# Where a unit's first copy, its last result and the last output piece stand in their queues

## The chip, the core and the metric

The kernel runs on one core of one Trainium2 chip. Time is device time of one execution in microseconds (us). TensorE (PE) multiplies, VectorE (DVE) does elementwise arithmetic on two operands, ScalarE (ACT) does activation functions and plain copies, GpSimd (POOL) and SyncE (SP) here mostly issue DMA transfers. Each engine runs its own queue in order and waits on semaphores for the others.

## The reference

The input is x of 2048 tokens by 512 channels, float32. With `ln` a layer norm without gain and `h`, `hh` a layer norm with gain and bias and the same shifted by one token:

```python
x = ln(L0_attn_x)                                  # first layer, RWKV
k = (h*mk + hh*(1-mk)) @ Wk.T;  v = (h*mv + hh*(1-mv)) @ Wv.T;  r = (h*mr + hh*(1-mr)) @ Wr.T
x = x + sigmoid(r) * wkv(k, v, tm_first) @ Wo.T    # 512 x 512 matrices
kk = (h*ck + hh*(1-ck)) @ Wkey.T                   # 2048 x 512
x = x + sigmoid((h*cr + hh*(1-cr)) @ Wcr.T) * (silu(kk) @ Wval.T)
y = L0_attn_x + x                                  # second layer, gated FFN
gate, up = split(ln(y) @ w_gate_up.T)              # 2 x 2048 rows
out = y + (silu(gate) * up) @ w_down.T
```

Almost all of it is matrix products of 512-wide blocks.

## The kernel before

**Tiling.** Tokens come in four blocks of 512. A weight of 512 x 512 and a block of 512 tokens form one 512 x 512 x 512 product, a *unit*. It is not multiplied in eight quarter products but in seven, by a Strassen-Winograd scheme: quarters A11..A22 of the weight and sums S1..S4 of them, quarters B11..B22 of the activations and sums T1..T4. A quarter product is eight matmuls of 128x128 by 128x256; the profile counts them on line 546.

**One unit** (`unit`, L526). Three accumulators of one PSUM bank each take the products: `z`, `accv`, `accx`. Step 1 puts A11·B11 into `z`, and ACT copies it to `accv` (L564). Step 2 adds A12·B21 to `accv`, which is result (0,0), and `sink` uses it. Step 6 adds S2·T2 to `z`, copied to an SBUF tile `u2` (L574). Step 5 adds S1·T1, copied to `accx` (L578). Then step 7 (S3·T3, result (1,1) from `z`), step 3 (`accx`, result (0,1)) and step 4 (A22·T4; DVE adds `z` and `u2` for result (1,0)). `sink` differs by unit: an activation on ACT for gates, k, r and the hidden layers, an addition or a multiplication on DVE for the others.

**Interleaving of units.** Steps 7, 3 and 4 are *held* and popped between the next unit's steps, so PE's order around a unit's start is: step 5 of the unit before, step 4 of the one before that, **step 1 of this unit, step 7 of the unit before, step 2 of this unit**. Step 2 adds to `accv`, so it can't start before the ACT copy of step 1 has ended; one product lies between them.

**Order of the other engines.** PE, DVE and ACT run in the order in which the program text emits. After each product, `due` runs the functions that were `put_off` (`later(fn, n)` runs fn at the n-th `due`), and `tick` (L290) spends the length of the product (STEP, 1.72) on work from the lists `hot`, `background` and `preps`: norms, mixes (`mix<-hT`, an ACT scaling on L483 and a DVE step on L387), sums of activations (L379) and sums of weights (`raw`). What `tick` emits stands in the queues at that point.

**The FFN's down product** (`down_product`, L1114) takes the scheme twice: seven outer products n = 0..6, each of them seven inner products of four groups (`steps`, L1150; matmuls of 128x128 by 128x128 on L1165). Inside one outer product, `z` is one 128-column piece of a bank that accumulates A11·B11, S2·T2, S1·T1, S3·T3 and A22·T4; after each of the first four, `keep` (L1177) lets ACT copy it to an SBUF tile `r`, and the next product into `z` must wait for that copy. `y` takes A12·B21 and S4·B22. `rest` (L1200) and `seventh` (L1211) finish `r` on DVE; `summed` (L1117) adds the outer products up. Inner products six and seven of outer product n are held and popped after the first and the second inner product of n + 1. For the last token block `sink` (L1243) adds a 128x2x256 piece to the residual tile and SP stores it; the piece (1,0) is first given its other terms at n = 5, and at n = 6 the last one, then stored as one 256 KB transfer.

The program ends when that last store has landed.

Of the kernel before, what the change touches and what calls it, by code (L numbers as in the profile page):

```python
# [11 lines left out]
ALU = mybir.AluOpType  # L12
# [3 lines left out]
P = 128  # L16
# [4 lines left out]
HB = TB // 2  # L21
# [38 lines left out]
def rwkv_ffn_kernel(  # L60
# [145 lines left out]
    def later(fn, ticks=1):  # L206
        put_off.append([ticks - 1, fn])
# [76 lines left out]
    def due():  # L284
        for item in put_off:
            item[0] -= 1
        while put_off and put_off[0][0] < 0:
            put_off.popleft()[1]()

    def tick(length=STEP):  # L290
        for item in preps:
            item[1] -= 1
        slack[0] = max(min(slack[0] + SHARE * length - spent[0], 2.5), -2.5)
        spent[0] = 0.0
        credit[0] = min(credit[0] + credit[1], 2.0)
        while slack[0] > 0 and (hot or background or preps):
            go = False
            if preps and credit[0] >= 1 and prep_one():
                credit[0] -= 1
                go = True  # L300
            elif hot or background:
                go = run_one(False)
            slack[0] -= spent[0]
            spent[0] = 0.0
            if not go:
                break

    def push(name, gen, ready=None):
        background.append([ready, gen, name, False, background])
# [68 lines left out]
    def tt(out, a, b, op):  # L378
        nc.vector.tensor_tensor(out, a, b, op)  # L379
        cost(size(out))  # L380
# [145 lines left out]
    def unit(weights, Bs, sink, by_token, done=None, free=None, loose=False):  # L526

        acc, tmp = {}, {}  # L530
        last = len(weights) - 1

        def product(z, a, b, first=False, between=None, part=None):
            if first:
                acc[z] = bank()
            pz = acc[z]
            groups = list(range(last + 1) if part is None else part)
            for g in groups:
                wg = weight(weights[g], a)
                act = Bs[g][b]  # L540
                for m in range(2):
                    for k in range(2):
                        lo = slice(m * P, (m + 1) * P)
                        lhsT = act[:, k, lo] if by_token else wg[:, k, lo]
                        rhs = wg[:, k, :] if by_token else act[:, k, :]
                        mm = nc.tensor.matmul(  # L546
                            pz[:, m, :],
                            lhsT=lhsT,
                            rhs=rhs,
                            start=first and g == 0 and m == 0 and k == 0,  # L550
                            stop=g == last and k == 1,
                            skip_group_check=True,
                        )
                latest[:] = [mm.ins.name]
                due()
                if g < groups[-1]:
                    tick()
                    if between is not None and g < 2:
                        between()

        def step1():
            product("z", A11, B11, True, pop_held)
            acc["v"], acc["x"] = accv, accx
            nc.scalar.copy(accv, acc["z"])  # L564

        def step2(part=None):
            product("v", A12, B21, part=part)
            if part is None or last in part:
                sink(0, 0, accv)

        def step6():
            product("z", S2, T2)
            tmp["u2"] = u_tile("u2")
            nc.scalar.copy(tmp["u2"], acc["z"])  # L574

        def step5():
            product("z", S1, T1)
            nc.scalar.copy(accx, acc["z"])  # L578
            if loose:
                tmp["u4"] = u_tile("u4")  # L580
                nc.scalar.copy(tmp["u4"], acc["z"])
            later(lambda: tt(tmp["u2"], tmp["u2"], accx, ALU.subtract), 1)

        def step7():
            if loose:
                product("y", S3, T3, True)
                tt(tmp["u4"], acc["y"], tmp["u4"], ALU.add)
                sink(1, 1, tmp["u4"])
                return
            product("z", S3, T3)  # L590
            sink(1, 1, acc["z"])

        def step3():
            product("x", S4, B22)
            sink(0, 1, accx)

        def step4():
            if loose:
                tt(tmp["u2"], tmp["u2"], tmp["u4"], ALU.add)
            product("z", A22, T4, loose)  # L600
            tt(tmp["u2"], acc["z"], tmp["u2"], ALU.add)
            sink(1, 0, tmp["u2"])
            if free is not None:
                free()
            if done is not None:
                later(done, 2)

        if last > 0:

            def most():  # L610
                step2(range(last))

            def rest():
                step2([last])

            order = (step1, None, most, step6, rest, step5)
        else:
            order = (step1, None, step2, step6, None, step5, None)
        for s in order:
            if s is None:  # L620
                pop_held()
            else:
                s()
                tick()
        held.extend(((STEP, step7), (STEP, step3), (STEP, step4)))
        if loose:
            release()
            flush()
# [485 lines left out]
    def down_product(b, sink, final):  # L1114
        base = {}

        def summed(n, r):  # L1117


            def add(o, i, j=None):  # L1120
                tt(base[o], base[i], r if j is None else base[j], ALU.add)

            if n == 0:
                base["p1"] = r
            elif n == 1:
                base["p3"] = r
            elif n == 2:
                base["u2"] = r
                add("u2", "u2", "p1")
            elif n == 3:  # L1130
                add("p1", "p1")
                sink(0, 0, base["p1"])
            elif n == 4:
                base["u4"] = r
                add("u4", "u4", "u2")
                add("p3", "p3", "u4")
                sink(0, 1, base["p3"])
            elif n == 5:
                add("u4", "u4")
                sink(1, 1, base["u4"])  # L1140
                add("u2", "u2")
                if final:
                    sink(1, 0, base["u2"])
            elif final:
                sink(1, 0, r, True)
            else:
                add("u2", "u2")
                sink(1, 0, base["u2"])

        def steps(n):  # L1150
# [25 lines left out]
            def keep(n, m):  # L1176
                nc.scalar.copy(st["r"][:, m, n * P : (n + 1) * P], st["z"])  # L1177
# [18 lines left out]
            def fifth():  # L1196
                product(st["z"], S1, T1, False)
                keep(0, 1)

                def rest():  # L1200
                    r = st["r"]
                    tt(r[:, 0, P:], r[:, 0, P:], r[:, 1, :P], ALU.subtract)
                    tt(r[:, :, :P], st["y"], r[:, :, :P], ALU.add)

                later(rest, 1)

            def sixth():
                product(st["z"], S3, "T3", False)
                keep(1, 1)

            def seventh():  # L1211
                product(st["z"], A22, T4, False)
                r = st["r"]
                tt(r[:, 0, P:], st["z"], r[:, 0, P:], ALU.add)
                if n + 2 < 7:
                    quarter_sums(b, n + 2)
                summed(n, r)
# [4 lines left out]
        for n in range(7):  # L1222
            t = DOWN[n][1]
            while (b, t if t != T3 else "T3") not in made:
                flush_one()
            one = steps(n)
            one[0]()
            tick(half)
            pop_held()
            one[1]()  # L1230
            tick(half)
            pop_held()
            for k in range(2, 5):
                one[k]()
                tick(half)
                if n == 0:
                    pop_held()
            held.extend((half, k) for k in one[5:])

    def ffn_down(b):  # L1240
        final = b == NB - 1

        def sink(i, j, c, last=False):  # L1243
            v = block_view(rs[b], i, j)
            tt(v, c, v, ALU.add)
            if final and (i, j) == (1, 0) and not last:
                return
            eng = nc.sync if final else nc.gpsimd
            eng.dma_start(  # L1249
                out_t[b][:, 2 * j : 2 * j + 2, i * HB : (i + 1) * HB],  # L1250
                rs[b][:, 2 * j : 2 * j + 2, i * HB : (i + 1) * HB],
            )

        down_product(b, sink, final)

# [157 lines left out]
```

## Time and profile before

| | |
|---|---|
| median of 3 runs | 1256.92 us (1256.81 to 1257.21) |
| profiled execution, its own time | 1256.11 us |
| its span on the core | 1254.3 us |
| TensorE clock granted | 1.0 throughout |
| ACT copies `accv<-ps` (L564) | 64, 571 ns each |
| ACT copies `u<-ps` (L574), `accx<-ps` (L578) | 64 each, 585 and 571 ns |
| DVE `TENSOR_TENSOR` 128x512 | 685 to 692 ns |
| DVE `TENSOR_TENSOR` 128x128, 128x256 | 289 to 292 ns, 425 ns |
| ACT `ACTIVATE` 128x512 from an SBUF tile, from PSUM | 630 ns, 597 ns |
| last store, 256 KB, issue to landing | 2.2 us |

The span is the time between the first and the last instruction; 1.8 us of the profiled execution lie outside it. A row of a timeline gives start, duration, engine, line, operation, output and inputs, and in brackets how long the engine had been idle and who released it. Ends of matmuls are modelled by the profiler, so distances between matmuls are taken here from start to start.

### The profile page before, as it was taken

The page shows a single profiled execution, that of the slowest core. Times are in us where ns is not written, and L with a number is a line of the kernel's source. Part 1 is how long each engine was busy: PE and PEld are TensorE (multiplying, and loading weights), DVE is VectorE, ACT ScalarE, POOL GpSimd, SP SyncE. Part 2 cuts the span into 40 slices and gives each one's busy share as a digit, 9 for nine tenths or more (in the row PEclk, how much of TensorE's full clock was granted, in tenths as well). Part 3 has the DMA queues.
Part 4 walks back from the last instruction along what each step waited for, and adds up shares of the span by engine and source line. Part 5 has one row for each costly group of instructions (what it writes and reads, how often), then busy time and mean ns, then how long its engine had stood idle before and what let it go on. Part 6 is the DMA issues. An engine that isn't in the chain of part 4 may idle for free.

```text
span 1254.3 us, 18161 instructions
## 1 busy us (share of the span) xinstructions
PE 1238.0 (99%) x6588; PEld 1109.2 (88%) x6588; DVE 702.6 (56%) x1319; ACT 355.8 (28%) x656; POOL 151.1 (12%) x276
## 2 busy tenths in 40 slices
PE   8999999999999999999999999999999999999998
PEld 7888888888888888888888888998899988998898
DVE  5867566467674665722562265555546455462466
ACT  5433263142522334302311232212221132212211
POOL 2122221222121222222210000000000000000000
PEclk9999999999999999999999999999999999999999
DMA  5666777888778877798865655895559855785575
GB/s 188 233 195 211 244 249 244 249 292 282 241 259 257 290 251 248 248 334 309 254 211 178 221 145 151 247 345 164 144 173 302 280 151 150 234 291 165 152 220 200
DMA packets 137959, 288.55 MB, mean 230 GB/s; under 512 B 17296, under 2 KB 18320, under 8 KB 136848
## 3 DMA queue, kind: packets, MB, share of 16 engines
q1 hardware_dynamic: 115424, 215.53, 56.1%
q0 software_dynamic: 21440, 70.27, 15.4%
q10 hardware_dynamic: 1008, 1.59, 0.3%
q8 instruction: 53, 0.87, 0.3%
q14 instruction: 34, 0.28, 0.1%
HBM read 245.39 MB, written 41.94 MB: 229 GB/s over the span
## 4 chain that ended last, share of the span: by engine, by line
PE 95%; ACT 3%; DVE 2%; issue 1%; DMA 0%; POOL 0%; ACTq 0%; DVEq 0%; POOLq 0%
PE ps L546 49%; PE ps L1165 14%; PE accv L546 11%; PE accx L546 10%; PE ps L656 8%; PE ps L430 2%; ACT mix L483 1%; PE warm L337 1%; DVE u L379 1%; DVE mix L387 0%; DMA w<-in_w 0%; ACT e L877 0%; ACT x L740 0%; ACT r L878 0%; ACT accv L564 0%
## 5 line engine op out<-in xcount | busy, mean ns | idle before, releaser
L546 PE MATMUL ps<-zT,w 128*128 128x256 f32 x1280 | 289.5, 379 | 0.7 <-ACT u L574 0.7
L546 PEld LDWEIGHTS ps<-zT,w 128*128 128x128 f32 x1280 | 241.8, 190 | 33.2 <-ACT u L574 1.1
L546 PE MATMUL ps<-mix,w 128*128 128x256 f32 x880 | 201.0, 379 | 0.0
L546 PEld LDWEIGHTS ps<-mix,w 128*128 128x128 f32 x880 | 167.0, 190 | 22.6
L379 DVE TENSOR_TENSOR u<-u,accx 128x512 f32<-128x512 f32 x64 | 43.9, 686 | 118.3 <-ACT accx L578 118.3
L1165 PE MATMUL ps<-w,hid 128*128 128x128 f32 x832 | 104.7, 275 | 0.4 <-ACT r L1177 0.4
L1165 PEld LDWEIGHTS ps<-w,hid 128*128 128x128 f32 x832 | 99.8, 192 | 1.3 <-ACT r L1177 0.5
L546 PE MATMUL ps<-w,t 128*128 128x256 f32 x432 | 96.5, 379 | 0.0
L546 PEld LDWEIGHTS ps<-w,t 128*128 128x128 f32 x432 | 81.9, 190 | 11.1
L1165 PE MATMUL ps<-w,quads 128*128 128x128 f32 x704 | 89.2, 275 | 0.4 <-ACT r L1177 0.4
L656 PE MATMUL ps<-mix,w 128*128 128x256 f32 x384 | 85.1, 380 | 3.7 <-DVE mix L387 3.7
L656 PEld LDWEIGHTS ps<-mix,w 128*128 128x128 f32 x384 | 72.3, 190 | 14.6 <-DVE mix L387 5.1
L1165 PEld LDWEIGHTS ps<-w,quads 128*128 128x128 f32 x704 | 84.3, 192 | 0.9 <-ACT r L1177 0.5
L379 DVE TENSOR_TENSOR u<-ps,u 128x512 f32<-128x512 f32 x65 | 44.9, 691 | 66.3 <-PE ps L546 66.3
L578 ACT COPY accx<-ps 128x512 f32<-128x512 f32 x64 | 36.5, 571 | 153.0 <-PE ps L546 152.9
L379 DVE TENSOR_TENSOR raw<-raw 128x512 f32<-128x512 f32 x92 | 63.3, 688 | 29.1 <-DMA raw<-d 10.0
L564 ACT COPY accv<-ps 128x512 f32<-128x512 f32 x64 | 36.5, 571 | 140.5 <-PE ps L546 140.5
L1177 ACT COPY r<-ps 128x128 f32<-128x128 f32 x112 | 29.8, 266 | 142.7 <-PE ps L1165 142.7
L574 ACT COPY u<-ps 128x512 f32<-128x512 f32 x64 | 37.5, 585 | 112.9 <-PE ps L546 112.9
L1249 POOL DMA_DIRECT2D out<-resid x12 | 8.6, 716 | 476.9 <-DVE resid L379 476.9
L546 PE MATMUL accv<-zT,w 128*128 128x256 f32 x256 | 60.7, 380 | 0.7 <-ACT accv L564 0.7
L546 PE MATMUL accx<-zT,w 128*128 128x256 f32 x256 | 60.5, 379 | 0.0
(158 smaller groups left out, 1659.1 us busy)
## 6 DMA issues: line engine op xcount, KB each, us to landing
w<-sum SPq DMA_DIRECT2D x304, 256.0 KB, 3.3
w<-in_w SPq DMA_DIRECT2D x256, 256.0 KB, 3.3
w<-dd SPq DMA_DIRECT2D x112, 256.0 KB, 3.6
raw<-in_w POOLq DMA_DIRECT2D x48, 256.0 KB, 4.8
sum<-raw POOLq DMA_DIRECT2D x48, 256.0 KB, 3.8
w<-d SPq DMA_DIRECT2D x48, 256.0 KB, 3.3
q<-in_w POOLq DMA_DIRECT2D x36, 256.0 KB, 4.9
sum<-q POOLq DMA_DIRECT2D x36, 256.0 KB, 3.9
```

The costliest lines, as they stand in the source:

```text
L337: nc.tensor.transpose(pt[:, 0, 0:P], ident, ident)
L379: nc.vector.tensor_tensor(out, a, b, op)
L430: nc.tensor.transpose(flat[:, t * P : (t + 1) * P], h[:, t, c * P : (c + 1) * P], ident)
L483: nc.scalar.activation(dst(c), hT[:, c, 0:TB].rearrange("p (j t) -> p j t", j=2), AF.Copy, scale=onem[:, row - MK, c : c + 1],)
L546: mm = nc.tensor.matmul(pz[:, m, :], lhsT=lhsT, rhs=rhs, start=first and g == 0 and m == 0 and k == 0, stop=g == last and k == 1, skip_gro ...
L564: nc.scalar.copy(accv, acc["z"])
L574: nc.scalar.copy(tmp["u2"], acc["z"])
L578: nc.scalar.copy(accx, acc["z"])
L656: mm = nc.tensor.matmul(acc[i, j][:, m, :], lhsT=act[:, k, lo] if by_token else wg[:, k, lo], rhs=wg[:, k, :] if by_token else act[:, k, : ...
L1165: mm = nc.tensor.matmul(dst, lhsT=x[k][:, g, :], rhs=wt[:, g, :], start=first and g == 0, stop=g == 3, skip_group_check=True,)
L1177: nc.scalar.copy(st["r"][:, m, n * P : (n + 1) * P], st["z"])
L1249: eng.dma_start(out_t[b][:, 2 * j : 2 * j + 2, i * HB : (i + 1) * HB], rs[b][:, 2 * j : 2 * j + 2, i * HB : (i + 1) * HB],)
```

## The change

In `unit`: `product` gets an argument `read`, called when the last matmul of the product has been emitted and before `due`; step 1 hands in the copy to `accv`, which thus stands on ACT's queue ahead of everything that `due` runs. Step 4 no longer calls `sink(1, 0, ...)` itself, but puts it off to the next product's `due`, that is behind the copy. Step 4 also sets a flag, `quiet`, and the next `tick` takes nothing from `background`.

In the down product, only for the last block and n = 6: the third inner product (S2·T2) is emitted ahead of the held seventh of n = 5, and then the fifth (S1·T1) ahead of the fourth (S4·B22). `seventh` adds `r` to the output tile before its own product and stores three quarters of the piece; after its product one addition of 128x128 takes `z` straight from PSUM into the last quarter, which is stored.

```diff
+    quiet = [False]
     def tick(length=STEP):
...
-            elif hot or background:
+            elif hot or background and not quiet[0]:
                 go = run_one(False)
...
+        quiet[0] = False
...
-        def product(z, a, b, first=False, between=None, part=None):
+        def product(z, a, b, first=False, between=None, part=None, read=None):
...
                 latest[:] = [mm.ins.name]
+                if read is not None and g == groups[-1]:
+                    read()
                 due()
...
         def step1():
-            product("z", A11, B11, True, pop_held)
             acc["v"], acc["x"] = accv, accx
-            nc.scalar.copy(accv, acc["z"])
+            product(
+                "z", A11, B11, True, pop_held, read=lambda: nc.scalar.copy(accv, acc["z"])
+            )
...
             product("z", A22, T4, loose)
             tt(tmp["u2"], acc["z"], tmp["u2"], ALU.add)
-            sink(1, 0, tmp["u2"])
+            later(lambda: sink(1, 0, tmp["u2"]), 1)
             if free is not None:
                 free()
             if done is not None:
                 later(done, 2)
+            quiet[0] = True
...
                 if final:
-                    sink(1, 0, base["u2"])
-            elif final:
-                sink(1, 0, r, True)
+                    sink(1, 0, base["u2"], "first")
...
             def seventh():
+                r = st["r"]
+                if final and n == 6:
+                    sink(1, 0, r, "most")
                 product(st["z"], A22, T4, False)
-                r = st["r"]
+                if final and n == 6:
+                    sink(1, 0, st["z"], "last")
+                    return
                 tt(r[:, 0, P:], st["z"], r[:, 0, P:], ALU.add)
...
-            pop_held()
-            for k in range(2, 5):
+            if final and n == 6:
+                one[2]()
+                tick(half)
+                pop_held()
+                order = 4, 3
+            else:
+                pop_held()
+                order = 2, 3, 4
+            for k in order:
                 one[k]()
                 tick(half)
...
+        eng = nc.sync if final else nc.gpsimd
+        def store(tokens, cols):
+            eng.dma_start(out_t[b][:, tokens, cols], rs[b][:, tokens, cols])
-        def sink(i, j, c, last=False):
-            v = block_view(rs[b], i, j)
+        def sink(i, j, c, part=None):
+            tokens, cols = slice(2 * j, 2 * j + 2), slice(i * HB, (i + 1) * HB)
+            if part == "last":
+                tokens, cols = 0, slice(HB + P, 2 * HB)
+            v = rs[b][:, tokens, cols]
             tt(v, c, v, ALU.add)
-            if final and (i, j) == (1, 0) and not last:
-                return
-            eng = nc.sync if final else nc.gpsimd
-            eng.dma_start(
-                out_t[b][:, 2 * j : 2 * j + 2, i * HB : (i + 1) * HB],
-                rs[b][:, 2 * j : 2 * j + 2, i * HB : (i + 1) * HB],
-            )
+            if part is None or part == "last":
+                store(tokens, cols)
+            elif part == "most":
+                store(1, cols)
+                store(0, slice(HB, HB + P))
```

More of the change, by code (lines that the diff above doesn't have):

```diff
@@ L1198, in fifth, with rest @@
                 keep(0, 1)
-                def rest():
-                    r = st["r"]
-                    tt(r[:, 0, P:], r[:, 0, P:], r[:, 1, :P], ALU.subtract)
-                    tt(r[:, :, :P], st["y"], r[:, :, :P], ALU.add)
                 later(rest, 1)
+            def rest():
+                r = st["r"]
+                tt(r[:, 0, P:], r[:, 0, P:], r[:, 1, :P], ALU.subtract)
+                tt(r[:, :, :P], st["y"], r[:, :, :P], ALU.add)
             def sixth():
@@ L1211, in seventh @@
             def seventh():
+                r = st["r"]
+                if final and n == 6:
+                    sink(1, 0, r, "most")
                 product(st["z"], A22, T4, False)
-                r = st["r"]
+                if final and n == 6:
+                    sink(1, 0, st["z"], "last")
+                    return
                 tt(r[:, 0, P:], st["z"], r[:, 0, P:], ALU.add)
```

## The prediction

> **What bounds the kernel now.** First the busy shares:
>
> ```profile
> PE 1238.0 (99%) x6588; PEld 1109.2 (88%) x6588; DVE 702.6 (56%) x1319; ACT 355.8 (28%) x656; POOL 151.1 (12%) x276
> ```
>
> PE is never free for long, and the number of matmuls doesn't change. So the change can gain only where PE waits, and behind its last matmul. The waits of PE, longest first (total us, times, longest):
>
> ```profile
> PE accv L546 <- ACT accv L564: 3.8, 5, 1.0
> PE ps L656 <- DVE mix L387: 3.7, 4, 1.5
> PE ps L546 <- issue: 1.6, 1, 1.6
> PE warm L337 <- POOL ident masks.py:199: 1.4, 1, 1.4
> PE ps L1165 <- ACT r L1177: 0.7, 2, 0.4
> PE ps L546 <- ACT u L574: 0.7, 1, 0.7
> ```
>
> The first row is what the copy to `accv` costs: five waits in 64 units. Rows 2 to 4 lie before 112 us, where plain units and the start run; nothing is moved there. The fifth is the end of the program. No row names a DMA. I then looked at each of the five in the timeline. PE alone around the second:
>
> ```profile
> 261.40 7.07 PE L546 MATMUL ps<-mix,w 128*128 128x256 f32 x32
> 269.48 1.99 PE L546 MATMUL accv<-mix,w 128*128 128x256 f32 x8 [1.01 <-ACT accv L564]
> 271.31 1.89 PE L546 MATMUL ps<-mix,w 128*128 128x256 f32 x8
> ```
>
> and ACT alone at the same place:
>
> ```profile
> 266.43 0.63 ACT L877 ACTIVATE e<-r 128x512 f32<-128x512 f32 x1 [2.14 <-DVE r L383]
> 267.09 0.63 ACT L878 ACTIVATE r<-r 128x512 f32<-128x512 f32 x1
> 267.62 1.32 ACT L483 ACTIVATE mix<-hT_b,onem 128x512 f32<-128x512 f32 x2
> 268.85 0.57 ACT L564 COPY accv<-ps 128x512 f32<-128x512 f32 x1
> 269.37 1.32 ACT L483 ACTIVATE mix<-hT_b,onem 128x512 f32<-128x512 f32 x2
> ```
>
> The four products from 261.40 are step 5, step 4, step 1, step 7. Step 1 is done near 266.6, but the copy stands behind two exponentials (the result (1,0) of step 4, which waits for DVE) and two background mixes, and starts at 268.85. PE starts 0.06 us after its end: it is the copy that is waited for.
>
> **The unit part, step by step.** A product goes start to start in 1.727 us (256.22 to 261.40 is three of them). From the start of step 5 to the start behind step 2 are five products, 8.635 us if nothing stalls. Measured:
>
> - 161.77 to 171.59: 9.82, lost 1.19 (copy behind a silu that waited for DVE's `u`)
> - 261.40 to 271.31: 9.91, lost 1.28 (above)
> - 324.86 to 333.87: 9.01, lost 0.37 (silu)
> - 337.32 to 346.38: 9.06, lost 0.42 (silu)
> - 424.10 to 434.01: 9.91, lost 1.28 (exponentials and mixes, as above)
>
> Together 4.54 us, more than the 3.8 of the waits view since a stall also delays the weight load behind it.
>
> With the copy directly behind its product it waits only for PE. A copy starts 0.20 us behind the start of the following product (273.03 to 273.23 for `u`). In the second case step 1 ends at 261.40 + 3 x 1.727 = 266.58, the copy runs 266.78 to 267.35, and step 2 wants it at 268.31: 0.96 spare. In the first, third and fifth cases the same 0.96 holds, ACT being free at 165.1, 329.3 and 427.0; in the fourth three mixes end at 342.6 and the copy at 343.3, wanted at 344.2. So all five stalls go: **-4.54**.
>
> What is now late instead:
>
> - *The result (1,0) on ACT, in every unit.* The copy waits at the head of ACT's queue until step 1 has ended, and the activation stands behind. Counted from the end of step 4: copy 1.93 to 2.50, activation to 3.13 (0.63). The next ACT reader, step 7's result, is ready at 3.65. It fits with 0.5 spare; the activation's own reader (the next unit's multiplication, or sums of hidden quarters) is products away. Price 0.
> - *Background work held back one tick.* In the two long k/r/v stretches (from 262 and from 425 us) the mixes come behind the copy, and DVE does three or four mixes before the step that multiplies the exponentials, up to 2 us later than now. I followed DVE through with 0.6 to 0.75 per step. At 425 us the last v result (`e<-u,e`) ends near 454.2 and the second sum near 455.5, on a scale where PE is 1.28 earlier; the output unit wants them at 455.2 and 456.9. Spare 1.0 and 1.4; in the stretch from 262 us about 1.7 and 2. DVE has about 4 us of idle time between 429 and 453 that absorbs the delay. Price 0, at most 1 each if I am off by a DVE step or two.
> - *Sums of weights and of `zT`.* They move by one or two places on DVE, have tens of us, and GpSimd's order is unchanged; SP's is unchanged until the last block. Price 0.
>
> The units with no held steps (681.80 and 686.19) wait for a copy with nothing between; those stay.
>
> **The end, step by step.** The timeline now:
>
> ```profile
> 1243.12 1.95 PE L1165 MATMUL ps<-w,quads 128*128 128x128 f32 x16
> 1244.22 0.29 DVE L379 TENSOR_TENSOR r<-ps,r 128x128 f32<-128x128 f32 x1 [0.33 <-PE ps L1165]
> 1246.67 0.69 DVE L379 TENSOR_TENSOR resid<-r,resid 128x512 f32<-128x512 f32 x1
> 1247.21 1.16 PE L1165 MATMUL ps<-w,hid 128*128 128x128 f32 x8 [0.35 <-ACT r L1177]
> 1247.67 0.42 DVE L379 TENSOR_TENSOR r<-ps,r 128x256 f32<-128x256 f32 x1
> 1248.73 1.16 PE L1165 MATMUL ps<-w,quads 128*128 128x128 f32 x8 [0.35 <-ACT r L1177]
> 1249.92 0.29 DVE L379 TENSOR_TENSOR r<-ps,r 128x128 f32<-128x128 f32 x1 [1.83 <-PE ps L1165]
> 1250.32 0.69 DVE L379 TENSOR_TENSOR resid<-r,resid 128x512 f32<-128x512 f32 x1
> 1251.04 0.37 SPq L1249 DMA_DIRECT2D out<-resid  x1
> ```
>
> *PE:* inner products start 0.89 apart without a wait. S1·T1 now stands at 1245.80, S3·T3 waits for its copy until 1247.21 (0.52 lost), A22·T4 until 1248.73. With S4·B22 moved between S1 and S3 that first wait is covered: S1 1244.91, S4 1245.80, S3 1246.69, A22 1246.69 + 1.41 = 1248.10, its result 1.19 later, 1249.29. Each moved product also moves its weight load on SP's queue by one place (`w<-dd` ahead of `w<-d`); the ring of 12 tiles has them issued by 1237.95, five us before the first moved product at 1243, and loads land in 3.9 to 4.4 there, so that costs nothing.
>
> *DVE:* but n = 5's last product also comes one place later (1244.01 instead of 1243.12), and its five steps with `rest` shift by 0.89: the one at 1247.67 moves to 1248.56. Behind it the large addition starts at 1249.02 and, a dependent step of that size taking 0.73, the last one runs 1249.75 to 1250.04. DVE, not PE, is last; the 0.52 is hidden by it. Against 1251.01 now: 0.97 earlier.
>
> *SP:* the two early stores are issued from 1249.74. Consecutive issues stand 0.4 to 0.5 apart in the trace, so the third goes at about 1250.55, not 1250.07: 0.49 before today's 1251.04.
>
> *Landing:* the store of 256 KB landed in 2.2 us, and the windows of one us show its data as 0.05 + 0.69 = 0.74 us of all engines. A quarter carries 0.19, so by the row it lands in about 1.65 and the end comes 1.04 earlier. Against splitting stands the Trainium skill, "DMA: Bandwidth & Descriptors", section "Bandwidth": batch transfers, since those under 64 KB are descriptor-dominated; its section on the anatomy of one DMA fits (for GpSimd's path) 2.0 us fixed plus bytes by 436 GB/s. By that fit 192 KB less save 0.45, and the end comes 0.94 earlier; if small size cost everything it saves, 0.49. No row shows a 64 KB store with 512-byte runs. Ends: 0.2 (it lands late behind its two neighbours) and 1.4 (SP issues faster, DVE not in the way); I take **-0.8**, nearer to the row.
>
> **Sum:** -4.54 - 0.8 = -5.3. The profiled execution becomes 1256.11 - 5.3 = 1250.8. The median of the runs shown is 0.8 above it, so 1256.92 - 5.3 = **1251.6** is what I forecast.
>
> **Rivals.**
>
> - *The end gains nothing* (three stores instead of one, landing late): 1256.92 - 4.5 = 1252.4. For it: SP is last in my sum. Against: its data are short. 12%.
> - *Part is given back*: DVE is late for the output units of the last two blocks by more than the spare 1.0 and 1.7 us; each us over is one us of PE, up to 1 and 2: 1253 to 1254.5. For it: my walk through DVE is a sum of many steps. 8%.
> - *The gain is taken back by transfers*: PE arrives 4.5 us earlier at stretches paced by DMA, so only their end counts: 1256.1 to 1256.9. For it: in 1234 to 1240 us DMA is over 0.9 busy. Against: SP waits for PE there, PE never for DMA. 5%.
> - *Slower*: the same late DVE chain with nothing absorbed. Three steps of 0.75 ahead of the exponentials' product plus 2 us of late ACT work make 4.3 us; minus the spare 1.0 and 1.7 that is 3.3 + 2.6 = 5.9 us of PE waiting for `e` and `t`, against 5.3 gained: 1257.5, and with one more mix each 1259. It decides from 4 us of lateness in each stretch on. Against it stand DVE's idle 4 us. 3%.
>
> That the change doesn't do what it says I exclude: in ACT's new order the copy is first in all five places, and nothing but step 1 and long finished readers of `accv` holds it.
>
> **How the numbers follow.** The forecast has 72%, its own range 1250.8 to 1252.4. The first rival falls at its edge, the second reaches to 1254.5; 1250.1 to 1253.9 leaves out about 2 in 10. The measurement can tell about 0.2%, 2.5 us, from no change: faster is forecast, first rival and second, 92%; within it the third, 5%; slower 3%.
>
> **What would show it.** Right: the row `PE accv <- ACT accv` falls to one wait near 0.7 (the unit at 681 us); the copies near 266 and 429 us start 0.2 behind the next product; the last DVE step is 128x128 from `ps` and ends about 1 us earlier against the last matmul than now; the last store is issued right behind two others. Wrong: new rows of PE waiting for DVE `e` or `t` in the output units, PE waiting for ACT `u`, or a last store that takes over 2.2 us.

## The result and the profile after

The changed kernel takes 1250.36 us, median of 6 runs (1249.98 to 1251.58); beside it the kernel before took 1256.66 (1255.65 to 1257.21). The ratio is 0.9952, 95% interval 0.9939 to 0.9965. The profiled execution took 1250.48 with a span of 1248.7, 5.6 shorter than before.

**What the span is made of.** PE begins with 44 warm-up matmuls (`warm`). They take 6.91 us before and 6.87 after, but 6.36 to 7.97 in the executions shown below, and everything behind starts later by as much. So this document splits each span at two points: the start of the first block product on PE (`ps<-mix,w` x24, 12.00 us before) and the start of the first inner product of n = 6 in the down product (1240.44 before, 1235.86 after), called the reference point below. The middle stretch holds the units. The end stretch runs to the end of the span, here from the time stamps of the traces (1254.34 before, 1248.70 after), since the views print it with one digit.

| kernel | median us | ratio, 95% interval | warm-up and start | middle | end |
|---|---|---|---|---|---|
| before | 1256.66 | | 12.00 | 1228.44 | 13.90 |
| after | 1250.36 | 0.9952 (0.9939 to 0.9965) | 11.96 | 1223.90 | 12.83 |
| e1, end only | 1255.32 | 0.9990 (0.9983 to 0.9997) | 12.86 | 1228.46 | 12.83 |
| e2, unit only | 1251.67 | 0.9959 (0.9945 to 0.9974) | 11.96 | 1223.90 | 13.91 |
| e3, no quiet tick | 1250.93 | 0.9953 (0.9938 to 0.9968) | 11.63 | 1223.90 | 12.83 |
| e4, quiet tick only | 1253.08 | 0.9972 (0.9960 to 0.9983) | 11.44 | 1226.00 | 12.84 |
| e9, copy twice | 1253.48 | 0.9976 (0.9967 to 0.9985) | 13.07 | 1226.31 | 12.84 |
| e10, copy four times | 1314.18 | 1.0461 (1.0446 to 1.0475) | 12.81 | 1287.44 | 12.84 |
| e5, old order at the end | 1249.92 | 0.9952 (0.9937 to 0.9966) | 11.63 | 1223.91 | 12.46 |
| e6, last piece as one store | 1251.10 | 0.9958 (0.9943 to 0.9973) | 12.44 | 1223.91 | 13.05 |
| e7, early stores from ACT | 1250.48 | 0.9954 (0.9939 to 0.9969) | 12.29 | 1223.91 | 12.53 |
| e8, copy waits covered | 1250.14 | 0.9949 (0.9933 to 0.9966) | 12.89 | 1223.90 | 12.08 |
| e11, e8 with e7 | 1249.15 | 0.9944 (0.9931 to 0.9958) | 13.02 | 1223.90 | 11.77 |
| e12, e11 with one store back on SP | 1249.24 | 0.9943 (0.9926 to 0.9960) | 12.87 | 1223.90 | 11.74 |

Where the edits leave a stretch alone, the middle repeats to 0.02 us and the end to 0.01. By these stretches the change gave 4.54 us in the units and 1.07 at the end.

PE's waits after the change (total us, times, longest; the four rows left out are as before: three lie before 112 us, and the wait of 0.7 for ACT's `u` is that of a unit without held steps, now at 681.62):

```profile
...
PE accv L549 <- ACT accv L569: 0.7, 1, 0.7
PE ps L1171 <- ACT r L1183: 0.4, 1, 0.4
```

The row of the copy has fallen from 3.8 us in five waits to one wait of 0.7, the unit without held steps at 677 us. The row at the end (ACT `r`) has one wait instead of two. No row of PE waiting for `e`, `t` or a DMA has come in, and PE's busy time hardly moves (1238.0 before, 1236.4 after). ACT and PE at the second of the five places:

```profile
265.56 0.57 ACT L569 COPY accv<-ps 128x512 f32<-128x512 f32 x1 [2.49 <-PE ps L549]
266.04 0.63 ACT L885 ACTIVATE e<-r 128x512 f32<-128x512 f32 x1
...
267.24 1.32 ACT L486 ACTIVATE mix<-hT_b,onem 128x512 f32<-128x512 f32 x2
```
```profile
260.18 7.07 PE L549 MATMUL ps<-mix,w 128*128 128x256 f32 x32
267.08 1.89 PE L549 MATMUL accv<-mix,w 128*128 128x256 f32 x8
268.81 1.89 PE L549 MATMUL ps<-mix,w 128*128 128x256 f32 x8
```

The copy now stands ahead of the two exponentials and the mixes. ACT idles 2.49 us in front of it, and PE released it. From 260.18 to 268.81 are five products in 8.63 us: nothing is lost. At the other four places the same stretch also takes 8.63.

The end, DVE and SP (SP's first row merges its three issues; the second is the third issue alone):

```profile
1243.98 0.42 DVE L382 TENSOR_TENSOR r<-ps,r 128x256 f32<-128x256 f32 x1
1244.51 0.69 DVE L382 TENSOR_TENSOR resid<-r,resid 128x512 f32<-128x512 f32 x1
1245.30 0.29 DVE L382 TENSOR_TENSOR resid<-ps,resid 128x128 f32<-128x128 f32 x1
```
```profile
1245.23 1.32 SPq L1265 DMA_DIRECT2D out<-resid  x3
1246.14 0.41 SPq L1265 DMA_DIRECT2D out<-resid  x1
```

The large addition now stands ahead of the last one. The last ends at 1245.59, but SP, still busy with the two early stores, issues the third only at 1246.14. The landing of the last one and of the early one of its size (KB each, us from issue):

```profile
out<-resid SPq DMA_DIRECT2D x2, 64.0 KB, 1.6
```

So the 1.07 at the end have three parts. The last issue stands 0.32 earlier (10.28 behind the reference point instead of 10.60). Its landing takes 1.60 instead of 2.21. And the span ends 0.96 behind the last landing, where it was 1.09 with the store of 256 KB; why that differs isn't known.

### The profile page after: what moved, and what is told of

The parts are those of the page before. It is cut to its first block, busy times and chain, and to the rows that moved or that the text cites. A ratio compares the mean times of both kernels' runs of the same rounds, so it can differ in the third digit from the quotient of the medians.

```text
span 1248.7 us, 18185 instructions
## 1 busy us (share of the span) xinstructions
PE 1236.4 (99%) x6588; PEld 1109.5 (89%) x6588; DVE 701.5 (56%) x1319; ACT 354.5 (28%) x656; POOL 151.1 (12%) x276
## 4 chain that ended last, share of the span: by engine, by line
PE 98%; ACT 1%; DVE 1%; issue 0%; POOL 0%; DVEq 0%; POOLq 0%
PE ps L549 53%; PE ps L1171 14%; PE accv L549 11%; PE accx L549 11%; PE ps L664 8%; PE ps L433 2%; PE warm L340 1%; ACT mix L486 0%; ACT mix L829 0%; ACT hT_a L821 0%; DVE resid L382 0%; DVE mix L390 0%; DVE r L382 0%; ACT e L885 0%; PE accx L346 0%
```

## The experiments: the two parts by themselves

**e1: the end without the units.** `product` no longer gets `read` in step 1, the copy follows `product`, step 4 calls `sink` itself, and `quiet` is never set; the down product stays changed.

> The kernel before with only the edits of the last block's end. Theory (five copies cost 4.5 us, the end 1.0): span 1254.3 - 1.0 = 1253.3, the five waits of PE for the copy still there. Rival (the end brings nothing, since three stores land later than one): 1254.3.

Its row of waits is the old one:

```profile
PE accv L549 <- ACT accv L569: 3.8, 5, 1.0
```

The middle is 1228.46, the end 12.83: the end part alone is worth 1.06, and touches nothing else. In the medians it is hardly above what they can tell.

**e2: the units without the end.** The functions `down_product` and `ffn_down` as before, all else as after.

> The kernel before with only the unit's edits (copy, put-off result, quiet tick). Theory: span 1254.3 - 4.5 = 1249.8, one wait of 0.7 for the copy left (the unit near 681 us). Rival (part of the stalls comes back as PE waiting for DVE's e or t in the output units): above 1250.8, with such rows in the waits of PE.

The middle is 1223.90, the end 13.91, so the units alone give 4.54, and the parts add up: 4.54 and 1.06 against 5.61 together.

## The experiments: which line of the unit part does it

**e3: without the quiet tick.**

```diff
-            quiet[0] = True
```

> The changed kernel without the quiet tick: ACT then has two background mixes ahead of the copy in the two long k/r/v stretches. Theory (ACT is idle there for 2.5 us before the copy and the mixes need 1.3): no stall, span as the changed kernel, 1248.7 within 0.3. Rival (the quiet tick is what removes the second and fifth stall): 2.5 more, 1251.2.

ACT at the second place:

```profile
263.50 1.34 ACT L486 ACTIVATE mix<-hT_b,onem 128x512 f32<-128x512 f32 x2 [0.74 <-PE ps L549]
265.23 0.57 ACT L569 COPY accv<-ps 128x512 f32<-128x512 f32 x1 [0.39 <-PE ps L549]
```

Two mixes are again ahead of the copy, but they run in the 2.49 us in which ACT idled: 1.34 us of work, and 0.39 us of idle time is left. The middle is 1223.90 as with the flag. The quiet tick isn't needed.

**e4: the quiet tick alone.** The copy behind `due`, `sink` called by step 4, the flag kept:

```diff
-            product(
-                "z", A11, B11, True, pop_held, read=lambda: nc.scalar.copy(accv, acc["z"])
-            )
+            product("z", A11, B11, True, pop_held)
...
+            nc.scalar.copy(accv, acc["z"])
...
-            later(lambda: sink(1, 0, tmp["u2"]), 1)
+            sink(1, 0, tmp["u2"])
```

> The changed kernel with the copy and the result (1,0) back in their old places, the quiet tick kept. Theory: in the second and fifth place the copy follows the two exponentials at once and ends about 0.1 us before it is wanted, so these stalls nearly go; the three silu stalls stay (1.19 + 0.37 + 0.42): span 1248.7 + 2.0 = 1250.7. Rival (the tick does nothing without the move): 1248.7 + 4.5 = 1253.2.

The waits (one of the three is the unit without held steps, and the one of 0.11 at the third place is not counted), and ACT at the fourth place:

```profile
PE accv L549 <- ACT accv L569: 1.7, 3, 0.9
```
```profile
341.60 0.63 ACT L970 ACTIVATE s<-u 128x512 f32<-128x512 f32 x1 [0.79 <-DVE u L382]
342.14 0.58 ACT L569 COPY accv<-ps 128x512 f32<-128x512 f32 x1
```

Here the copy stands behind a silu that waited for DVE's `u`. From start to start the three silu places lose 1.18, 0.37 and 0.42, the two with exponentials 0.06 each (8.69 against 8.63): 2.09, and the middle is 2.10 longer. So at the places with exponentials neither alone makes the copy late: the exponentials alone cost 0.06, the mixes alone (e3) nothing, both together 1.28. At the silu places it was the result that waits for DVE, and moving the copy ahead of it cures that. The move takes two lines, `read` and the put-off `sink`; by the order of the program text either alone leaves the result ahead of the copy, but neither was run alone.

**e9 and e10: how late may the copy be?** `read` does the copy two or four times over, which leaves the values as they are.

```diff
+            def read():
+                for _ in range(2):
+                    nc.scalar.copy(accv, acc["z"])
...
+            product("z", A11, B11, True, pop_held, read=read)
```

> The changed kernel with the copy to accv made twice in a row in each of the 64 units (same values). Theory (one product of cover, of which 0.96 is spare): the second copy ends at 0.2 + 2 x 0.6 = 1.4 behind the product, wanted at 1.73: nothing in 63 units, 0.6 in the one unit without cover: span 1248.7 + 0.6 = 1249.3. Rival (the spare is used up by other work on ACT): 20 us or more.

> The same with four copies. Theory: the fourth ends at 2.6, 0.9 later than wanted, and the first weight load behind the stall adds 0.1: 63 x 1.0 + 1.8 = 65 us: span 1314. Rival (PE has other slack behind the copy, so that only the units stall that stalled before): under 1260.

e9 missed: PE waits for the copy four times, not once. PE and ACT at one of the places that were not expected:

```profile
832.49 1.05 PE L1174 MATMUL ps<-w,hid 128*128 128x128 f32 x8
833.92 1.99 PE L549 MATMUL accv<-zT,w 128*128 128x256 f32 x8 [0.37 <-ACT accv L571]
```
```profile
832.69 1.17 ACT L571 COPY accv<-ps 128x512 f32<-128x512 f32 x2 [1.46 <-PE ps L549]
```

At 834, 977 and 1120 us the unit is the first behind a down product. What stands between step 1 and step 2 there is one of its inner products, of 0.89 us, not a product of 1.73. The copy has 0.96 - 0.84 = 0.12 to spare, and a second one of 0.60 makes PE wait 0.37, with 0.6 lost start to start as in the other stalls. Three times 0.60, and 0.60 more at the unit that waited already, are the 2.41 by which the middle is longer. The other 60 units carry a second copy for nothing. With four copies PE waits for nearly every unit (48.8 us in 59 waits), 0.74 to 0.79 in 55 of the 59, near the 0.84 that three further copies of 0.60 less the 0.96 of room make, and the middle is 63.5 us longer, 0.99 per unit. The copy was put where it belongs, but with little room in three places.

## The experiments: the end

**e5: the old order of inner products, the new split of the last piece.**

```diff
-            if final and n == 6:
-                one[2]()
-                tick(half)
-                pop_held()
-                order = 4, 3
-            else:
-                pop_held()
-                order = 2, 3, 4
+            pop_held()
+            order = 2, 3, 4
```

> The changed kernel with PE's old order of the last inner products, everything else of the end kept. Theory (DVE and SP set the end, not PE): the two early stores can go 0.4 us sooner, because n = 5's additions are 0.9 earlier, and the last addition stands where it is: span 1248.7 - 0.3 = 1248.4, in no case over 1248.9. Rival (PE's covered wait is worth its 0.5): 1249.2.

DVE at its end (the reference point lies at 1235.54):

```profile
1242.76 0.42 DVE L382 TENSOR_TENSOR r<-ps,r 128x256 f32<-128x256 f32 x1
1243.80 0.69 DVE L382 TENSOR_TENSOR resid<-r,resid 128x512 f32<-128x512 f32 x1 [0.62 <-ACT r L1183]
1245.02 0.29 DVE L382 TENSOR_TENSOR resid<-ps,resid 128x128 f32<-128x128 f32 x1 [0.52 <-PE ps L1171]
```

PE's last product starts 0.6 us later than after the change (8.28 behind the reference point against 7.67), and still the end comes 0.37 earlier. The last step of `rest` on DVE starts 0.90 earlier (7.22 behind the reference point against 8.12). Not all of that is gained: the large addition behind it now waits 0.62 for ACT's copy of S3·T3, the product whose wait on PE the new order covers, and ends 8.95 behind that point instead of 9.34. SP issues the early stores 0.39 earlier, and the third 0.38. So the new order takes 0.5 of waiting off PE and puts DVE 0.90 later; since DVE then comes last, the sum is a loss. With DVE out of the way PE's wait does count: it makes up most of the 0.62, and e8 takes both.

**e6: the last piece as one 256 KB store behind the last addition.**

```diff
-            if part is None or part == "last":
+            if part is None:
                 store(tokens, cols)
-            elif part == "most":
-                store(1, cols)
-                store(0, slice(HB, HB + P))
+            elif part == "last":
+                store(slice(0, 2), slice(HB, 2 * HB))
```

> The changed kernel with one store of 256 KB behind the last addition instead of three. Theory: it is issued 0.5 us sooner, since SP has no other issue before it, but lands in 2.2 instead of 1.6: span 1248.7 + 0.1 = 1248.8. Rival A (splitting is worth the whole 0.6 of landing): 1249.3. Rival B (batching is better): 1248.2.

SP's last issue:

```profile
1246.11 0.37 SPq L1265 DMA_DIRECT2D out<-resid  x1
```

It is issued 9.76 behind the reference point, 0.03 behind the last addition, where the split version's third waits for SP until 10.28. Its landing:

```profile
out<-resid SPq DMA_DIRECT2D x1, 256.0 KB, 2.2
```

It lands in 2.2 instead of 1.6. So splitting gains 0.6 in landing and gives 0.52 back in SP's queue, worth 0.1 by these rows. The stretch shows 0.22: the other 0.13 lie behind the landing (1.09 to the end of the span, as before, against 0.96).

**e7: the two early stores issued by ACT.** In the branch "most", `store(..., nc.scalar)` instead of SP.

> The changed kernel with the two early stores issued by ACT instead of SP, the last by SP. Theory (two issues of 0.44 stand before the last one on SP): the last store is issued at the end of the last addition, 0.5 sooner: span 1248.2. Rival (the last store waits for the data of the two before, or issues share one generator): 1248.7.

The end takes 12.53, 0.30 less, not the 0.5 that was expected. SP's store is issued at 9.76 behind the reference point and lands 0.5 sooner, but ACT's second one, issued at the same moment, takes 1.8 instead of 1.6 and lands 0.2 behind it.

**e8: S3's and A22's waits for a copy both covered.** For n = 6 the third inner product stands between the two held ones of n = 5, then come S1·T1, A12·B21, S3·T3 (no longer held) and S4·B22, with `rest` right behind it, and A22·T4 last:

```diff
             def fourth():
                 product(st["y"][:, 1, :], S4, B22, True)
+                if final and n == 6:
+                    rest()
...
-            one[1]()
-            tick(half)
             if final and n == 6:
                 one[2]()
                 tick(half)
                 pop_held()
-                order = 4, 3
+                order = 4, 1, 5, 3
```

> The changed kernel with the last inner products in the order A11, (n = 5: S3), S2, (n = 5: A22), S1, A12, S3, S4, A22, so that every copy of z has a product beside it and n = 5's last product keeps its old place. Theory: A22 ends 0.5 sooner, the large addition starts 0.8 sooner, SP's third issue is 0.8 sooner: span 1247.9. Rival (the landing alone sets the end): 1248.7.

DVE at the end (the reference point lies at 1236.79):

```profile
1244.13 0.42 DVE L382 TENSOR_TENSOR r<-ps,r 128x256 f32<-128x256 f32 x1 [0.23 <-PE ps L1171]
1244.66 0.69 DVE L382 TENSOR_TENSOR resid<-r,resid 128x512 f32<-128x512 f32 x1
```

The large addition follows `rest` without a wait for ACT's copy, 7.87 behind the reference point, where it stood at 8.65 after the change and at 8.26 in e5. The end takes 12.08, 0.76 less. The last addition ends 8.96 behind the reference point instead of 9.73, and the third issue, still behind two others on SP, moves by the same 0.8 (9.51 instead of 10.28).

**e11: e8 and e7 together.**

> The covered order of the last inner products together with the two early stores on ACT. Theory: the last addition ends about 0.85 sooner than in the changed kernel and its store is issued at once, 1.3 sooner in all: span 1247.4. Rival (one of the two is hidden behind the other): 1247.9 to 1248.2.

The end of e11 on all engines (rows left out where the dots are):

```profile
1244.27 0.42 DVE L382 TENSOR_TENSOR r<-ps,r 128x256 f32<-128x256 f32 x1 [0.23 <-PE ps L1171]
...
1245.52 0.84 ACTq L1267 DMA_DIRECT2D out<-resid  x2
1245.59 0.29 DVE L382 TENSOR_TENSOR resid<-ps,resid 128x128 f32<-128x128 f32 x1
1245.91 0.34 SPq L1267 DMA_DIRECT2D out<-resid  x1
```

PE now waits for nothing, DVE in front of its last steps for PE alone, and SP issues 0.03 behind the last addition. The end stretch is 11.77, against 13.90 before (the 11.78 in the expectation of e12 comes from a span of one digit). It fell 0.2 short of what was expected. Of its landings, SP's store took 1.6, and ACT's second:

```profile
out<-resid ACTq DMA_DIRECT2D x1, 64.0 KB, 1.8
```
```profile
1245.92 0.45 ACTq L1267 DMA_DIRECT2D out<-resid  x1
```

ACT's second store goes out at 1245.92 and lands at 1247.71; SP's, issued at 1245.91, lands at 1247.51. The last to land is an early store.

**e12: that store back on SP,** ahead of the last one.

> As e11_covered_act, but of the two early stores only the 128 KB one is issued by ACT; the 64 KB one goes through SP, ahead of the last. Stretch from the first inner product of n = 6 to the end: e11 has 11.78, the changed kernel 12.84. Theory A (in e11 the end is set by ACT's second store: issued at 1245.94, landing 1.8 later, against 1245.91 plus 1.6 for SP's): ACT's only store now lands 0.4 earlier, SP's last is issued at about 0.05 behind the last addition's end, and the stretch is 11.55 to 11.65. Rival B (SP's own store sets the end, and a store in front of it on SP delays it by what remains of its issue step): 11.78 to 11.95. The stretch from the start to that inner product stays as in e11. Median 1249 to 1250, which the medians cannot tell from e11's.

It measured 11.74, between the two ranges. SP's last store is issued at 1245.80 and lands in 1.7, the 128 KB store on ACT in 2.0 instead of 1.8:

```profile
out<-resid ACTq DMA_DIRECT2D x1, 128.0 KB, 2.0
```

The store moved as theory A has it, but both queues start at the same moment now and each landing is 0.1 to 0.2 longer. Whether they slow each other wasn't tested; with 0.03 between e11 and e12 nothing was gained in this way. e11 and e12 are the fastest kernels here, 1.1 us ahead of the change in the end stretch; a median can't tell that from no change.

## Why the prediction was right

- *The stalls.* "Together 4.54": the middle is 4.54 shorter, all five gone. The part rests on start to start distances. The reading of the waits view beside it was wrong: its five waits are not the five places. It counts the 0.66 at 681.80, which stays, and leaves out the 0.11 at 332.04. The five places hold only 3.2 us of idle time on PE; each cost 0.26 to 0.28 more than its wait. By that view the gain would have been put 1.3 too low.
- *What is late instead costs nothing.* Right, and with more room than worked out. At 425 us `e<-u,e` ends 1.8 us ahead of its reader (1.0 was predicted), the second sum 2.2 (1.4); in the stretch from 262 us 1.8 (1.7) and 2.2 (2). The walk through DVE, with 0.6 to 0.75 per step, erred on the safe side. So the rivals that lived on a late DVE had no start.
- *Weight loads.* "In 3.9 to 4.4" missed the two issued last, at 1237.06 and 1237.95 before: they took 5.4 and 5.2. It cost nothing: no row of PE waiting for a DMA came in.
- *The end, on PE, DVE and SP.* In the clock of before (plus 4.58) the last product stands at 1248.11 (predicted 1248.10), the last addition at 1249.88 (1249.75) and the third issue at 1250.72 (1250.55). DVE needed 0.13 more in two steps between dependent instructions of different size.
- *The landing.* "In about 1.65" by the row; it was 1.6. A quarter of the bytes landed 0.61 sooner, where the row gave 0.55 and the fit of the Trainium skill ("DMA: Bandwidth & Descriptors", the anatomy of one DMA) gives 0.45, an estimate for GpSimd's path. The page's warning (section "Bandwidth") that transfers under 64 KB are descriptor-dominated showed in no landing here, where none was under 64 KB; what splitting cost stood in SP's queue, 0.52 in e6.
- *The end's sum.* It came to 1.07; the row's sum was 1.04, the fit's 0.94, and -0.8 was taken. This was the mis-sized term, by 0.27: the row of this kernel's own store was nearer than the value set between it and an end that no row spoke for. That the row's sum fits so well is in part luck: the third issue came 0.17 later than worked out, the landing was 0.06 shorter, and 0.13 fell away behind the landing, which the prediction didn't ask about.
- *The median.* It was put at 1251.6, from a median 0.8 above the profiled execution. The profiled execution came 0.3 below its 1250.8, which is the end; but the median stands at 1250.36, 0.1 below the profiled one. So 0.9 of the 1.2 by which the median came out lower lies in how far single executions differ, most likely in the warm-up (only the profiled ones have a trace), which the prediction took as fixed. The median lies below the forecast's own range (1250.8 to 1252.4), and only 0.3 inside the wide one (from 1250.1).
- *What the prediction did not ask.* It saw that the moved product makes DVE late and that PE's wait is hidden by it, but not that the old order would then be better. e5 and e8 show it: 0.37 of the end was left lying with the old order, 0.76 with both waits covered.

The rival in which the end gains nothing falls with e1 and e2, the one in which transfers take the gain back with the table: the middle keeps all 4.54 of it.

## What to carry to other kernels

When PE is 99% busy, look for the few waits that are left and ask what stands ahead of the instruction that ends them on its in-order engine; move that one instruction up, and measure its room at the place with the shortest cover, not at the usual one. At a program's end, work back from the last landing through the issuing queue to the engine in front of it: covering a wait on another engine brings nothing if it makes that engine later (e5), and an early store in the same queue can cost the last one most of what its smaller size gains (e6). Compare short stretches between fixed points instead of whole spans when parts are smaller than what varies at the start.

## What the runs showed of the hardware

Apart from the edits, the spans differ between executions almost only in the warm-up. The 44 matmuls of 128x128 at the start, in the runs with the shortest and the longest warm-up: e4,

```profile
1.37 6.36 PE L340 MATMUL warm<-ident 128*128 128x128 f32 x44 [1.37 <-POOL ident masks.py:199]
```

and e9:

```profile
1.38 7.97 PE L340 MATMUL warm<-ident 128*128 128x128 f32 x44 [1.38 <-POOL ident masks.py:199]
```

Five us of the later part of the start in e4 and of the early part in e9 (window, its length, PE busy and count of matmuls of this size, granted clock, DMA share and GB/s):

```profile
5.00:10.00 5.00, 5.00 (x47) 1.00 1.06 386
```
```profile
2.00:7.00 5.00, 5.00 (x26) 1.00 0.94 342
```

A count takes in the two or three matmuls that reach into the stretch; from start to start they stand 109 to 112 ns apart in e4's stretch and 213 in e9's. In every run the distance halves in one step, 2.8 us after the first matmul in e4, 6.2 in e9 and in between in the others, although the granted clock reads 1.00 throughout. The 3.4 us between the two extremes, spent at half the rate, make 1.6 us, and the warm-ups differ by 1.6. The Trainium skill, "TensorE: Matmul & The Clock Gate", Part 1, describes this as a gate that opens after a busy window of about 3.4 us which runs free of the program. A gate that opens up to one window later, with half the rate meanwhile, would cost up to 1.7 us by that page, an estimate. The half rate and the spread agree with the page; in e4 the step comes earlier than a whole window after the first matmul. That the gate is the cause is not tested here.
